# Loading the first two sequences in rows, loading layer weights behind the first projections, and a new order of units

## The chip, the core and the metric

The kernel runs on one core of a Trainium2 chip. A core has TensorE (PE, matmuls; PEld is its weight load), VectorE (DVE), ScalarE (ACT), GpSimd (POOL) and SyncE (SP), which run side by side and wait for one another through semaphores. Here SP and ACT issue all DMAs, each in its own program order. The metric is the device time of one execution in microseconds; the kernel before took 3423.85 us (median of 3 runs, 3422.1 to 3424.76).

## The reference

The inputs are 32 sequences `x` and 32 side sequences `fside`, each 256 tokens by 256 features, and a length per sequence. All is float32.

```
# conditioning: cross attention, 16 heads of 16
q = (fside + b_self) @ Wq + bq
k = concat(x + b_prev, fside + b_self) @ Wk + bk
v = concat(x, fside) @ Wv + bv
score of q against x's keys, masked by the length; one more score: q with its own key
y = (softmax(scores / 4) over both @ v) @ Wo + bo
# two layers, 8 heads of 64, local windows of 128
h = shift(y); q, k, v = split(h @ wqkv)
q, k = l2norm(q) * q_scale, l2norm(k) * k_scale, turned by rotary tables
y = y + local_attention(q, k, v) @ wo
h = layernorm(shift(y)) * lg + lb;  a, g = split(h @ w1 + b1)
y = y + (a * gelu(g)) @ w2 + b2
out = x + y
```

`shift` takes the second half of the features from the token before.

## The kernel before, in words

**Tiling.** Two sequences make a group (`G` = 2), so there are 16 groups. Activations lie with features on the 128 partitions and tokens along the row. `stream` (two buffers, L766) holds the running `y` of a group with a column of zeros in front, so that the shift is an offset.

**Stages of a group.** The loop at the end of `tile_kernel` makes, for each group and each of its sequences: `load_sequence` (L697) with `blocks` (L691), which loads `fside` and `x` with four DMAs each in blocks of 32 by 32, whose runs are 128 bytes; `prepared` (L874), which turns the two tiles on VectorE (stream transposes, 32 by 32), projects q, k, the own score and the values (`cq`, `ck`, `cs`, `vals`, `self`), and spreads q and k over the partitions into `qh` and `kh` by eight DMAs each (`spread`, L889), with four small DMAs for the mask (`behind`); `conditioned` (L945): scores `S`, their maxima `mx` on VectorE (16 reductions a sequence), the maxima turned (`nmT`) and written into `qh` as rows, transposed scores `ST`, exponentials `eT` on ACT, the weighted values `AV`, then `ohT`, `at` on POOL, `turn` and `co`. Then twice `attention` (L1042; `q`, `k`, `v`, `qkT`, `sc`, `ex`, `exT`, `av`, `wout`) and `feedforward` (L1226; `mean`, `var`, `rs`, `w`), and `finished` (L1334), which adds `x` and stores. `S`, `ST`, `sc` and others use PE in tiles of 32 or 64 rows; `AV`, `av` and some others in tiles of 32 or 64 columns; some matmuls are cut into halves or quarters of their columns (`parted`, L543) so that PE need not change its tile size.

**Weights.** Before the loop all weights are loaded on ACT's queue: the conditioning's (`wq`, `wk`, `wv`, biases, the table `misc` with the identity `ident`, L704 to L723), then sequence 1 (L769), then `wo` and both layers (L773 to L844). The layers' part also multiplies the rotary table `rope0` with the scales into `rope1`, `rope2` (VectorE), copies the ends of `w1` into `w1t` (POOL), and adds `lb @ w1` to `b1` by matmuls with one column (`b` on PE, tile `pb`, 44 rows of the trace a layer).

**What sets the order.** The code does not issue instructions as it runs. Each engine call is recorded as a node (`Plan.record`, L233), matmuls in units (`unit`, L194) with their tiles of five pools (SBUF `t2`, `t4`, `e6`, `sm`, and the eight PSUM banks) . `Plan.run` (L294) then simulates the engines with written costs and picks, whenever PE is free, the ready unit with the lowest score (`policy`, L1399). The score contains the unit's `stand`: its group times 215, its place, and a shift from the tables `SHIFT`, `FIRST` (group 0) and `FINAL` (the last two groups), which were found by search. The other engines take the ready node by `rank` (L538), that is by the time it became ready. `issue` (L552) writes the instructions in that order; they all carry line 567. So a new table or a new cost moves instructions throughout the program. A DMA's cost in the plan is its issue, its bytes on a shared wire and a landing of 2.2 us.

Of the kernel before, what the change touches and what calls it, by code (L numbers as in the profile page):

```python
# [19 lines left out]
P = 128  # L20
S = 256
D = 256
G = 2
# [3 lines left out]
FH, FD = 8, 64  # L27
# [130 lines left out]
class Plan:  # L158
# [15 lines left out]
    def __init__(self, tc, engines, pools, make):  # L174
        self.tc, self.engines, self.pools, self.make = tc, engines, pools, make
        self.nodes, self.units, self.unit_, self.group, self.place = [], [], None, 0, 0.0
        self.stage, self.stages, self.done = 0, {}, set()


    def tile(self, pool, name, shape):  # L180
# [113 lines left out]
    def run(self, policy):  # L294
# [13 lines left out]
        for u in self.units:  # L308
            for tiles in u.takes.values():
                for t in tiles:  # L310
                    t.lead = u.cost if t.lead is None else t.lead
                tiles.sort(key=lambda t: t.lead)
        self.idle = self.switches = self.cold = self.wire = 0.0

        def put(n):
            if n.engine == "PE":
# [40 lines left out]
        while todo:  # L357
# [12 lines left out]
            if e != "PE":  # L370
                ready = [n for n in waiting[e] if n.ready <= t]
                n = min(ready, key=lambda n: self.rank(n, e))
                waiting[e].remove(n)
                cost = n.cost
                if e == "S" and n.table not in ("any", None, self.table):
                    self.table, cost = n.table, cost + 1.3
                now[e] = t + cost
                if not n.load:
                    self.backlog[e] -= n.cost
                order.append(n)  # L380
                todo -= 1
                end = t + cost
                if n.load:
                    self.wire = max(self.wire, end) + n.load
                    end = self.wire + self.LANDING
                ended(n, end)
                continue
            fit = {u: fits(u) for u in units if u.ready <= t}
# [148 lines left out]

    def rank(self, n, e):  # L538
        other = e == "S" and n.table not in ("any", None, self.table)
        return n.ready + 2.0 * other, n.number  # L540


    def parted(self, u):  # L543
# [29 lines left out]
class Engine:  # L573
# [12 lines left out]


SHIFT = [
    156, 528, 54, -76, 49, 292, -28, 245, 120, -102, -425, 52, -30, 35, 68, 22, 33, 22, -208,
    -4, 119, -41, 61, 69, 90, 152, 19, 32, -62, -238, 52, -2, 49, -168, 13, -85, -54, -65, 36,  # L590
    64, 112, -439, -349, -167, 223, -408, -5, 62, -46, -234, 56, -27, 119, -7, -45, 96, -17,
    -38, 61, -374, -335, -58, 1, -150, -372, -152, -51, -265, -409, 8, 67, -53, 114, -41, -17,
    -83, 34, 68, 48, 60, -261, -99, -7, -76, -335, -100, -105, -191, -306, -58, 15, -102, 32,
    -23, -66, 39, -309, -188, 106, -258, 33, -30, -139, 22, -141, 82, -290, -255, 32, 19, -99,
    134, 126, 14, -15, -222, -574, -156, 97, 93, -32, -241, 50, 152, -118, -41, -45, 21, -102,
    20, 47, 3, 15, 55, 169, -56, -24, 43, 199, -247, 143, -97, -15, -223, -41, -95, -88, -212,
    -127, -29, -32, -285, -545, -142, -265, -8, -118, -6, 152, 84, -122, 25, 14, 4, 18, 141, 60,
    166, -454, -139, 25, -127, -186, -20,
]
FIRST = [  # L600
    0, 0, 0, 0, 0, 0, 0, 0, 10, 35, -9, 213, 102, 95, 210, -345, -65, -122, -290, 49, -201, 6,
    -193, -61, -7, 106, 99, -6, -100, -16, 106, 13, 65, -266, -137, 7, -58, 247, 58, 69, 48, 1,
    -114, -155, -32, -173, -34, 65, 135, 130, -117, 69, 71, 117, 272, 156, 73, -3, -1, -31, -33,
    -133, 51, 151, 175, 239, 445, 215, 231, 120, 135, 97, -3, -90, -188, -357, -32, -64, -276,
    -297, -374, -330, -535, -346, -72, -135, -217, 156, 27, 182, 40, -174, -48, 77, -252, -118,
    -307, -246, 33, -96, -400, -238, -150, -69, -239, 6, 79, 152, 26, -38, -60, -358, -15, -155,
    89, -99, -69, -60, 87, -3, -114, -222, -118, 60, -143, -246, -29, -171, -319, -115, -49,
    -17, -96, -75, -88, 113, 144, -56, -6, 35, -9, -141, -41, -74, -183, -115, -131, -49, -79,
    109, -65, -145, 55, -88, -244, -157, -153, -264, -181, -118, -121, -82, -23, -37, -86, -83,
    -110, -213, -219, -209, -160, -63, 0, 0,  # L610
]
FINAL = [
    0, 0, 0, 0, 0, 0, 0, 0, 56, -34, 24, 16, 12, 140, -55, -63, -14, 1, -33, -84, -66, -53, -46,
    -145, -40, -121, 67, -19, -32, -29, 98, 97, 8, 45, -119, -130, -61, -106, 67, 94, -33, 8,
    54, 33, 8, -94, -222, -47, -210, -95, -90, -11, -121, 156, 49, 10, 43, 87, 7, 64, -144, -81,
    35, -80, 47, -31, -76, -182, 53, 86, 32, 67, 229, 49, 115, 31, 6, -10, -135, 40, 27, -79,
    -83, -8, 108, -110, 63, -40, -249, -98, -95, -18, -170, -139, -28, -12, -41, 76, 83, 116,
    59, -9, 65, -157, -74, -50, -119, -145, -16, -25, 13, 6, 73, -2, -181, -184, -151, -49, -97,
    116, -8, 56, 187, 15, 69, -31, -42, -59, 109, 161, 193, 112, 209, 211, 117, 80, 41, 59, 77,
    -84, 136, 47, 92, -54, 145, 66, 93, 1, -60, 152, -30, 108, 108, -119, 50, -9, -29, -39, 44,  # L620
    -113, -118, -128, -103, 66, 10, -89, -27, -49, -2, -10, 53, 34, -67, -8,
]


# [1 line left out]
def tile_kernel(ctx: ExitStack, tc: tile.TileContext, a: dict, out: bass.AP):  # L626
# [64 lines left out]
    def blocks(name, src):  # L691
        t = sb2(name, P, 2, S // 32, 32)
        for i in range(4):
            ld(t[32 * i : 32 * i + 32], blocked(src)[i])
        return t

    def load_sequence(n, after=()):  # L697
        plan.unit(after=after)
        loaded[n] = [blocks(name, src[n]) for name, src in (("ft", f), ("xt", x))]

    load_sequence(0)
    plan.unit()

    def weight(name, src, cols):  # L704
        t = kept(name, (P, 2, cols))
        ld(t, src.rearrange("(c p) e -> p c e", p=P), act)
        return t

    wq, wk, wv = (weight(f"w{n}", a[f"L0_cond_W{n}"], D) for n in "qkv")

    def column(src, name, cols):

        t = kept(name, (P, cols))
        ld(t, src.rearrange("(c p) -> p c", p=P), act)
        return t
# [2 lines left out]
    b_self = column(a["L0_cond_b_self"].rearrange("a b d -> (a b d)"), "b_self", 2)  # L718
    bq = column(a["L0_cond_bq"], "bq", 2)
    bk = column(a["L0_cond_bk"], "bk", 2)  # L720
    bv = kept("bv", (P, D))
    ld(bv, a["L0_cond_bv"].partition_broadcast(P), act)
    ld(misc, a["c_misc"][:, 0:C_IOTA], act)  # L723

    lens_i = kept("lens_i", (B, 1), I32)
    ld(lens_i, a["itok_B_18_1004"].rearrange("(b c) -> b c", c=1))
# [39 lines left out]
    stream = [kept(f"stream{i}", (P, 2, G, S + 1)) for i in range(2)]  # L766
    for t in stream:
        vec.memset(t[:, :, :, 0:1], 0.0)
    load_sequence(1)  # L769

    plan.unit()  # L773
    wo = weight("wo", a["L0_cond_Wo"], D)
    bo = column(a["L0_cond_bo"], "bo", 2)
    rope0 = sb2("rope0", P, 2, 4, FD)
    ld(rope0, a["c_rope"].rearrange("(t p) j d -> p t j d", p=P), act)
    wqkv, wout, w1, w1t, w2, rope, lg, lb, b1, b2 = ([] for _ in range(10))
    full = HID // P
    last = HID - full * P  # L780
    for l in range(DEPTH):
        wqkv.append(weight(f"wqkv{l}", a["L0_ffn_wqkv"][l], 3 * INNER))
        r = kept(f"rope{l + 1}", (P, 2, 4, FD))
        h = FD // 2
# [57 lines left out]
        for i in range(2):  # L842
            part = b1[l][:, i, 0 : NJ - i]
            vec.tensor_tensor(part, part, pb[:, i, 0 : NJ - i], ALU.add)  # L844

    def projected(name, w, j, src):
        plan.unit()
        pm = bank(name, P, S)
        for c in range(2):
            pe.matmul(  # L850
                pm,
                lhsT=w[:, c, j * P : (j + 1) * P],
                rhs=src[:, c, :],
                start=(c == 0),
                stop=(c == 1),
            )
        return pm
# [16 lines left out]
    def prepared(n, b):  # L874

        ft, xt = loaded.pop(n)
        plan.unit()
        fT, xT = sb2("fT", P, 2, S), sb2("xT", P, 2, S)
        for dst, src in ((fT, ft), (xT, xt)):
            vec.transpose(dst.rearrange("p c t -> p (c t)"), flat(src))  # L880
        for i in range(4):
            r = 32 * i + CD
            ld(
# [464 lines left out]
    for p in range(NG):  # L1348
        plan.group, plan.place = p, 0.0
        res = stream[p % 2]  # L1350
        heads, done = [], []
        for b in range(G):
            plan.stage = (p, 1 + b)
            n = G * p + b
            if n > 1:
                load_sequence(n, gates[p - 1][b : b + 1])
            heads.append(prepared(n, b))
        for b in range(G):
            plan.stage = (p, 3 + b)
            done.append(conditioned(b, *heads[b], res))  # L1360
        gates.append(done)
        for b in range(G):
            plan.stage = (p, 5, b)
            attention(0, b, res)
        plan.stage = (p, 6)
        feedforward(0, res)
        for b in range(G):
            plan.stage = (p, 7, b)
            attention(1, b, res)
        plan.stage = (p, 8)  # L1370
        late = feedforward(1, res)
        for b in range(G):
            plan.stage = (p, 9 + b)
            finished(G * p + b, b, res, (late,))
# [77 lines left out]
```

## Time and profile before

| | us |
|---|---|
| median of the runs | 3423.85 |
| the profiled execution | 3422.27 |
| its span, first to last instruction | 3420.5 |
| PE busy, of the span | 3348.6 |
| PE busy in the first 100 us | 73.30 |
| PE busy from 430 to 3000 us | 2550.82 of 2570 |
| PE busy from 3400 us to the end | 9.04 of 20.5 |
| mean granted PE clock, all; first 100 us | 0.990; 0.76 |
| DVE, ACT, POOL busy | 2161.9, 1780.5, 1163.4 |

The page gives the busy time of each engine, and the span in 40 equal slices with the busy share in tenths, the clock that PE was granted in tenths of full speed, and the DMA engines' share. A view of the waits names the waiting instruction, who released it, the total, the number of times and the longest. A view by windows gives busy time and number of instructions of PE, PEld, DVE, ACT and POOL in a stretch, then the clock, the DMA share and GB/s. A view in order of time gives start, duration, engine, operation, output and inputs, and how often in a row; queue names such as ACTq and SPq stand for the issue of a DMA. A float32 matmul has two rows in the trace, a transpose one; their ends are modelled, so what a row costs is read from the start of one to the start of the next.

### The profile page before, as it was taken

How to read it: one execution, taken by the hardware profiler on the slowest of the kernel's cores; microseconds unless marked ns; L12 is line 12 of the kernel's file. 1: busy time of each engine (PE TensorE's matmuls, PEld its weight loads, DVE VectorE, ACT ScalarE, POOL GpSimd, SP SyncE). 2: the span in 40 equal slices, each digit the busy share in tenths (PEclk: the TensorE clock that was granted, in tenths of full speed). 3: DMA queues.
4: the chain of work that ended last, by engine and by line, in shares of the span. 5: the costliest groups of instructions: out<-in, count | busy, mean ns of one | idle time of the engine just before them, and what ended most of it. 6: DMA issues, size and time to landing. Idle time of an engine off the chain costs nothing.

```text
span 3420.5 us, 69279 instructions
## 1 busy us (share of the span) xinstructions
PE 3348.6 (98%) x25984; PEld 1908.7 (56%) x25984; DVE 2161.9 (63%) x6673; ACT 1780.5 (52%) x4537; POOL 1163.4 (34%) x1195
## 2 busy tenths in 40 slices
PE   6999999999999999999999999999999999999998
PEld 5665556465564655656455564655646556465554
DVE  3558567485675747657485674847657486574763
ACT  0556456473554726456373563735547364554653
POOL 0325052250613407043160522507134070432541
PEclk7999999999999999999999999999999999999999
DMA  5100010010101001010010100101010010100001
GB/s 147 20 15 11 12 27 9 16 26 9 26 15 21 17 13 20 16 20 17 13 21 14 27 13 15 24 7 26 16 20 17 13 20 15 27 15 12 4 2 27
DMA packets 310926, 69.00 MB, mean 20 GB/s; under 512 B 286776, under 2 KB 308096, under 8 KB 310592
## 3 DMA queue, kind: packets, MB, share of 16 engines
q1 hardware_dynamic: 298848, 54.24, 9.3%
q10 hardware_dynamic: 11744, 10.34, 1.1%
q8 instruction: 207, 3.39, 0.4%
q14 instruction: 127, 1.04, 0.1%
HBM read 35.53 MB, written 8.39 MB: 13 GB/s over the span
## 4 chain that ended last, share of the span: by engine, by line
PE 77%; DVE 12%; POOL 3%; ACT 1%; issue 1%; POOLq 0%; SPq 0%; DMA 0%; DVEq 0%; ACTq 0%
PE w L567 27%; DVE ex L567 6%; PE wout L567 6%; PE q L567 5%; PE av L567 4%; PE k L567 4%; PE sc L567 4%; PE S L567 4%; PE v L567 3%; PE ST L567 3%; PE vals L567 3%; PE AV L567 3%; PE exT L567 2%; PE qkT L567 2%; DVE rot L567 2%; PE cs L567 2%
## 5 line engine op out<-in xcount | busy, mean ns | idle before, releaser
L567 ACT ACTIVATE ex<-ex,nm,rq 128x128 f32<-128x128 f32 (+1 forms) x1024 | 546.2, 537 | 107.3 <-DVE nm L567 106.1
L567 PE MATMUL w<-cen,w 128*128 128x512 f32 (+2 forms) x1480 | 589.2, 598 | 0.8 <-DVE cen L567 0.3
L567 POOL TENSOR_TENSOR raw<-raw,rot 128x512 f32<-128x512 f32 x256 | 327.6, 1281 | 749.2 <-DVE rot L567 660.3
L567 PEld LDWEIGHTS w<-cen,w 128*128 128x128 f32 (+2 forms) x1480 | 224.9, 175 | 270.7 <-issue 231.4
L567 DVE TENSOR_SCALAR ex<-ex,den 128x128 f32<-128x128 f32 (+1 forms) x1024 | 351.4, 457 | 5.2
L567 DVE TENSOR_REDUCE mx<-S 128x2 f32<-128x512 f32 x512 | 314.3, 686 | 49.4 <-PE S L567 49.3
L567 PE MATMUL w<-act,w 128*128 128x512 f32 (+3 forms) x880 | 324.6, 602 | 2.9 <-DVE act L567 2.8
L567 ACT ACTIVATE eT<-ST 128x512 f32<-128x512 f32 x512 | 263.8, 605 | 115.0 <-PE ST L567 109.8
L567 DVE CUSTOM_DVE_ANT_0 ex<-sc,misc 128x128 f32<-128x128 f32 (+1 forms) x1024 | 299.2, 353 | 31.3 <-PE sc L567 30.8
L567 DVE SCALAR_TENSOR_TENSOR act<-w,b,act 128x512 f32<-128x512 f32 (+1 forms) x192 | 143.4, 748 | 262.0 <-PE w L567 195.5
L567 ACT ACTIVATE act<-w,b 128x512 f32<-128x512 f32 (+1 forms) x192 | 128.9, 686 | 280.1 <-PE w L567 276.8
L567 POOL TENSOR_TENSOR xs<-stream 128x512 f32<-128x512 f32 x32 | 35.0, 1094 | 641.5 <-PE cs L567 318.1
L567 PE MATMUL wout<-qT,wout 128*64 128x256 f32 (+2 forms) x1728 | 242.8, 381 | 0.5 <-DVE nm L567 0.3
L567 PE MATMUL v<-wqkv,stream 128*128 128x512 f32 (+1 forms) x608 | 242.5, 599 | 0.0
L567 PE MATMUL k<-wqkv,stream 128*32 128x512 f32 (+2 forms) x1104 | 239.9, 593 | 0.0
L567 PE MATMUL q<-wqkv,stream 128*32 128x512 f32 (+2 forms) x960 | 237.7, 594 | 0.2 <-ACT stream L567 0.2
L567 ACT COPY exT<-exT 128x384 f32<-128x384 f32 x512 | 207.3, 498 | 54.5 <-PE exT L567 53.8
L567 PEld LDWEIGHTS w<-act,w 128*128 128x128 f32 (+3 forms) x880 | 124.8, 176 | 167.1 <-issue 151.5
L567 POOL TENSOR_TENSOR rq<-ss,minus_half 128x8 f32<-128x8 f32 x128 | 215.1, 1684 | 4.9
L567 POOL TENSOR_TENSOR ss<-ss,minus_half 128x8 f32<-128x8 f32 x128 | 213.3, 1666 | 5.7
L567 PE MATMUL sc<-kT,qT 64*128 64x128 f32 (+1 forms) x2048 | 205.7, 337 | 0.4
L567 PEld LDWEIGHTS wout<-qT,wout 128*64 128x64 f32 (+2 forms) x1728 | 161.6, 147 | 73.0 <-issue 17.6
(127 smaller groups left out, 5520.2 us busy)
## 6 DMA issues: line engine op xcount, KB each, us to landing
ft<-in_fside_BxSxS_dram SPq DMA_DIRECT2D x128, 64.0 KB
xt<-in_x_dram SPq DMA_DIRECT2D x128, 64.0 KB
qh<-qc SPq DMA_DIRECT2D x256, 32.0 KB
kh<-kc SPq DMA_DIRECT2D x256, 32.0 KB
ot<-in_x_dram SPq DMA_DIRECT2D x128, 64.0 KB
out_dram<-ot SPq DMA_DIRECT2D x128, 64.0 KB
wqkv<-in_L_ffn_wqkv_dram ACTq DMA_DIRECT2D x2, 1536.0 KB
w<-in_L_ffn_w_dram ACTq DMA_DIRECT2D x2, 1364.0 KB
```

Source lines behind the costliest of these rows:

```text
L567: ins = getattr(self.engines[n.engine], name)(*[real(v) for v in args], **{k: real(v) for k, v in kw.items()})
```

## The change

Sequences 0 and 1 (`n < G`) are loaded by one DMA for each tensor, in rows of 1 KB, and turned by PE (`turned_tiles`, four 128 by 128 transposes and a copy) instead of VectorE. The identity is loaded by a DMA of its own ahead of the other weights; `wv`, `bv` and the rest of `misc` come behind the small biases; sequence 1 is requested before the mask's inputs. Each layer's weights are recorded by a new function `load_layer(l, after)`, called for layer 0 behind the recording of sequence 0's projections and for layer 1 behind those of sequence 1, and with an edge that lets the plan start them only after these; `rope0` is loaded once for each layer. `wo` and `bo` are recorded behind this. In the plan a DMA now also waits for the landing of the one eight loads before it (`landed`), and `rank` has a term with the factor `hurry`, which the kernel sets to `HURRY` = 0.0 as before. The three tables of shifts are replaced; the number of units in group 0 has grown.

```diff
@@ Plan.run
+        self.landed = [0.0] * 8
...
                 if n.load:
-                    self.wire = max(self.wire, end) + n.load
+                    at = max(t, self.landed[-8]) + cost
+                    now[e] = at
+                    self.wire = max(self.wire, at) + n.load
                     end = self.wire + self.LANDING
+                    self.landed.append(end)
@@ Plan.rank
-        return n.ready + 2.0 * other, n.number
+        return n.ready + 2.0 * other + self.hurry * n.unit.stand, n.number
@@ SHIFT, FIRST, FINAL: other numbers throughout
@@ tile_kernel
+    def rows(name, src):
+        t = sb2(name, P, 2, D)
+        ld(t, src.rearrange("(t p) d -> p t d", p=P))
+        return t
     def load_sequence(n, after=()):
         plan.unit(after=after)
-        loaded[n] = [blocks(name, src[n]) for name, src in (("ft", f), ("xt", x))]
+        shape = rows if n < G else blocks
+        loaded[n] = [shape(name, src[n]) for name, src in (("ft", f), ("xt", x))]
     load_sequence(0)
     plan.unit()
+    ld(ident, a["c_misc"][:, C_ID : C_ID + P], act)
...
-    wq, wk, wv = (weight(f"w{n}", a[f"L0_cond_W{n}"], D) for n in "qkv")
+    wq, wk = (weight(f"w{n}", a[f"L0_cond_W{n}"], D) for n in "qk")
...
     bk = column(a["L0_cond_bk"], "bk", 2)
+    wv = weight("wv", a["L0_cond_Wv"], D)
     bv = kept("bv", (P, D))
     ld(bv, a["L0_cond_bv"].partition_broadcast(P), act)
-    ld(misc, a["c_misc"][:, 0:C_IOTA], act)
+    ld(misc[:, P:C_IOTA], a["c_misc"][:, P:C_IOTA], act)
+    load_sequence(1)
+    plan.unit()
...
-    load_sequence(1)
-    plan.unit()
-    wo = weight("wo", a["L0_cond_Wo"], D)
-    bo = column(a["L0_cond_bo"], "bo", 2)
-    rope0 = sb2("rope0", P, 2, 4, FD)
-    ld(rope0, a["c_rope"].rearrange("(t p) j d -> p t j d", p=P), act)
...
-    for l in range(DEPTH):
+    def load_layer(l, after):
+        plan.unit(after=after)
+        rope0 = sb2("rope0", P, 2, 4, FD)
+        ld(rope0, a["c_rope"].rearrange("(t p) j d -> p t j d", p=P), act)
         wqkv.append(weight(f"wqkv{l}", a["L0_ffn_wqkv"][l], 3 * INNER))
...
+    plan.unit()
+    wo = weight("wo", a["L0_cond_Wo"], D)
+    bo = column(a["L0_cond_bo"], "bo", 2)
@@ prepared
         ft, xt = loaded.pop(n)
-        plan.unit()
-        fT, xT = sb2("fT", P, 2, S), sb2("xT", P, 2, S)
-        for dst, src in ((fT, ft), (xT, xt)):
-            vec.transpose(dst.rearrange("p c t -> p (c t)"), flat(src))
+        if n < G:
+            fT, xT = turned_tiles("fT", ft), turned_tiles("xT", xt)
+            plan.unit()
+        else:
+            plan.unit()
+            fT, xT = sb2("fT", P, 2, S), sb2("xT", P, 2, S)
+            for dst, src in ((fT, ft), (xT, xt)):
+                vec.transpose(dst.rearrange("p c t -> p (c t)"), flat(src))
@@ the loop over groups
             heads.append(prepared(n, b))
+            if p == 0:
+                plan.stage = (-1, 1 + b)
+                load_layer(b, (plan.unit_,))
```

`turned_tiles` is in the kernel before (L859), where `conditioned` uses it for `at`.

## The prediction

> **What bounds the kernel now.** I read the page first, then what the engines waited for in the first 100 us, then the start in stretches of 2 us, then the start in order of time.
>
> ```profile
> span 3420.5 us, 69279 instructions
> ...
> PE 3348.6 (98%) x25984; PEld 1908.7 (56%) x25984; DVE 2161.9 (63%) x6673; ACT 1780.5 (52%) x4537; POOL 1163.4 (34%) x1195
> ...
> PE   6999999999999999999999999999999999999998
> ...
> PEclk7999999999999999999999999999999999999999
> DMA  5100010010101001010010100101010010100001
> ```
>
> TensorE (PE) is the bound, and only the first and the last slice leave it idle. Idle is 3420.5 - 3348.6 = 71.9 us: the stretches 0 to 100 and 430 to 3000 us show 73.30 and 2550.82 us busy, so 26.7 us of it fall in the first 100 us, 19.2 us in the 2570 us of the middle, and 11.5 us in the last 20.5 us. Nearly all that an edit of the start can win is in the first 100 us, whose waits are these:
>
> ```profile
> PE cq L567 <- DVE fT L567: 9.1, 1, 9.1
> PE bias L567 <- DMA bq<-in_L_cond_bq_dram: 7.8, 1, 7.8
> PE S L567 <- DMA w<-in_L_ffn_w_dram: 4.5, 1, 4.5
> PE S L567 <- DMA kh<-kc: 2.9, 1, 2.9
> PE self L567 <- DVE prod L567: 2.4, 2, 1.7
> ```
>
> Each line: who waited for what, total us, times, longest. The 9.1 us is for sequence 0 turned on VectorE, and the 7.4 us of "S" is for `qh` and `kh`, which SyncE spreads by 16 DMAs. The second loss there is the clock:
>
> ```profile
> 44.00:46.00 2.00, 2.00 (x10) 1.97 (x10) 0.00 (x0) 0.00 (x0) 0.00 (x0) 0.50 0.83 264
> 46.00:48.00 2.00, 0.06 (x1) 0.00 (x0) 0.27 (x2) 0.00 (x0) 0.00 (x0) 0.50 0.99 346
> 86.00:88.00 2.00, 2.00 (x20) 1.71 (x24) 0.74 (x2) 0.00 (x0) 0.00 (x0) 0.50 0.00 0
> ...
> 108.00:110.00 2.00, 2.00 (x12) 1.17 (x11) 0.00 (x0) 1.94 (x5) 0.00 (x0) 0.54 0.44 70
> ```
>
> The third number from the end is the granted clock: one half at 44 us although PE is busy throughout (matmuls with one column, for the b1 bias), and again at 86 us.
>
> **The front, part by part.** These rows of the start in order of time (start, us, engine, what, how many) give the prices:
>
> ```profile
> 22.09 3.78 PE L567 MATMUL cq<-fT,wq 128*128 128x256 f32 x8 [9.05 <-DVE fT L567]
> 25.67 1.32 PE L567 MATMUL vals<-wv,xT 128*128 128x256 f32 x4
> ...
> 33.71 0.39 ACTq L567 DMA_DIRECT2D wqkv<-in_L_ffn_wqkv_dram  x1
> ...
> 36.53 8.67 PE L567 MATMUL b<-lb,w 128*128 128x1 f32 x40
> ...
> 43.83 10.41 SPq L567 DMA_DIRECT2D kh<-kc  x8
> ...
> 70.22 5.03 SPq L567 DMA_DIRECT2D qh<-qc  x8
> ```
>
> *Loads in rows.* Removed: 16 DMAs of 32x16x32 (runs of 128 B) and four stream transposes of 0.66 to 0.71 us. Added: 4 DMAs of the shape of `wq`, which was issued at 0.72 and had released the next user of its semaphore at 3.98. The changed order puts them first on SP, so sequence 0 is there at about 4 us instead of 20. PE gets 16 transposes; 128 such rows in 22.4 us (turn) is 0.175 each: +2.8 us with their tails, 1.75 at the 109 ns from one to the next. VectorE gets four copies of 0.69 (aT<-turn), where it is idle. Both hide in the 7.8 us before "bias", which waits for `b_self`; that load is now issued at about 3.6 (behind the small `ident` load) and took 4.7 us before, so bias starts at 8.5, not 7.8, and takes the 5.3 us it took: 14 us. Then `cq` follows at once, not at 22.09: **8 us won here**.
>
> *Both sequences projected together.* 40 matmuls of 128x256 are 80 rows; four matmuls took 3.78 us at the slow start, others 0.216 us a row: 3.8 + 72 x 0.216 = 19.4, and two `self` units 1.8. PE has no more of this at 35 us. The first `spread` is of sequence 1: `qc` is complete at 21.3, then 8 + 4 + 8 DMAs at 0.63 (5.03 for 8, unloaded). But the 18th of them waits for a semaphore that the `rope` load took before it, and ACT issues that only behind its eighth projection copy, at 33.4; with the 3 us of a `wq` this gives 36.5, and with two more DMAs and 3.8 us of landing (the last `kh` issue ended at 54.24, S went on at 58.06), S starts at **41 us** (before: 50.60). PE idles 6 us for it.
>
> *The layers' weights later.* From the issue of `wqkv` to `w1` landed took 33.71 to 50.77 = 17.1 us for layer 1, and `w2` another 5.2. In the new order `wqkv` of layer 0 goes at 34.4, so `w1` lands at 51.5 and `w2` at 57. In the changed order a DMA of either queue waits for the one eight places before it, so the spreads of sequence 0 stand among these loads: its fifth `kh` waits for `w2`'s first part, two `qh` for b1 parts, one for the second `rope`. So SP goes on at 57, needs 10 more DMAs and a landing: S of sequence 0 at 67 us. Layer 1 follows: `w1` at 59.4 + 17.1 = 76.5, ACT free at 78.
>
> *What stands until ST.* S of sequence 1: 16 reductions `mx` at 0.62 from one to the next, from 43.2: 53, then 12 small rope products (1.5 us, which now stand before `nm`) and `nmT` at 55. The b1 bias of layer 0, 44 rows at one half: 8.67 + 0.99, so 9.5: 64.7. S of sequence 0 from 67: 2.2 + 9.8 + 1.5, `nmT` at 80.5. The bias of layer 1, 9.5 more, since PE stood nearly idle before: **ST starts at 90 us**. The kernel before starts ST at 85.88 with one S unit (1.15) and one `vals` unit (1.9 at full clock) still to do: 88.9. So the 8 us won at 14 us are spent by 90: VectorE paces both S blocks, and nothing but the bias lies beside them. **Front +1 us.** Ends: -9 if both bias units ran as at 69.24 (4.52 + 0.62) and S came sooner; +10 if the spreads land as late as under load (10.41 for 8).
>
> The Trainium skill, "TensorE: Matmul & The Clock Gate", Part 1 (The HAM clock gate), says that some 3.4 us of sustained matmuls bring the full clock. By it the bias units would be at full clock after that time, and ST would start some 5 us sooner. The row at 44 us differs: 8.7 us of one-column matmuls stayed at 0.50 to their end, so the sum goes by the row.
>
> *ST and AV of both sequences in one block.* Before, 86 to 118 us lost 1.9 us idle and 7.7 by the clock (4 in 86 to 94, 0.3, then 0.9 + 2 + 0.5 in 108 to 116). Now 8 ST and 8 AV units alternate in pairs: 128 rows each at 152.5/2048 and 143.6/2048 = 18.5 us of PE beside 32 exponentials at 263.8/512 = 16.5 us of ACT. I take half of the ST units at half clock (+4) and 2 us of waits: **-4 us** (-9 to +4: all at half clock).
>
> **The order anew, middle.** Counting the changed order of instructions: 63 of 1064 changes of tile size go (a 128x512 matmul is followed after 522 ns, not 429, by another tile size: 63 x 0.093 = -5.9). But `self` and `var` are cut less often into halves: 8 to 19 and 6 to 18 whole units, each about 0.5 us dearer (self: 9.0/8 against 13.8/23): +11. The 512 exT units stand 0.3 us further behind their scores than before, where 11 waits of 0.5 us stood: -4; `wout`, `vals`, `k` in larger tiles -3. **-2 us**, ends -8 and +13 (below).
>
> **The end.** Between 3000 and 3400 us PE waited 6.7 us, 2.8 of it for `act`, 1.6 at the last norm, where only two matmuls covered POOL's 1.02 us. The new order has three there, and no `w2` unit nearer than 1.7 us behind its `act` (before 0.8). After the last matmul the same 11.4 us follow: two VectorE adds, four transposes, POOL, eight output DMAs. **-2 us** (-5 to +3).
>
> Sum: +1 - 4 - 2 - 2 = -7. The profiled execution took 3422.27 us (span 3420.5 and 1.8 around it): 3415. Its runs have a median of 3423.85, 1.6 above: **3417 us**.
>
> **Rivals.** *Slower: the wait at `turn`.* PE now reaches `turn` 3.3 us of PE work behind `ohT` in 11 groups, before 4.4, and there `turn <- POOL at` waited 11 times 0.25 us (2.8 of the middle's waits). If POOL is as late as before, each costs 1.1 more: +12, and with the front at +5: 3433. It decides when `at` ends over 3.3 us after `ohT`. For it: the wait of each group is in the trace. Against: POOL was busy with other work until that `at`, and its order is new. *Slower: the load chain is late.* If each of the three waits of SP on `w2`, b1 and `rope` takes 5 us more, S of sequence 0 comes at 82 and ST at 105: +15, 3432; it decides from S after 75 us. For it: `kh<-kc` took 10.41 us beside weights and 5.77 us at 64.35, alone. Against: in the layer-1 stretch the weights took what I already count. *Given back:* the front stays +1, the ST block runs at half clock throughout, the middle is even: 3423. *Clock full in S and bias:* -9 in the front: 3407; for it the bias at 69.24, which ran behind 8 us of dense matmuls, against it the row at 44 us. That the rows do not hasten the first projection can hardly be: 4 DMAs stand where 16 stood.
>
> **How the numbers follow.** Forecast (3411 to 3421) 0.46; clock full 0.18; given back 0.13; `turn` 0.12; late chain 0.11. A measurement of this kernel can tell about 0.2% from no change, 6.8 us: faster is below 3417.0, slower above 3430.7. Of the forecast 0.28 lies below and 0.18 above; so faster 0.28 + 0.18 = 0.46, same 0.18 + 0.13 = 0.31, slower 0.23. The range, 3402 to 3433, leaves out the lower ends of front and middle together and the two slow rivals together.
>
> **What would show it.** `cq` at 14 us, S at 41, second S at 67, ST at 90; the clock one half in both bias units; the waits of the first 100 us on `fT` gone and new ones on `kh` and `mx`; `turn <- POOL at` below 0.5 us a group. Wrong if ST starts before 80 or after 100 us, or if the middle's idle time leaves 12 to 27 us.

## The result, and the profile after

The changed kernel takes 3458.18 us (median of 4 runs, 3456.87 to 3459.23), the kernel before beside it 3423.47. The ratio is 1.0101, 95% interval 1.0084 to 1.0119: slower by 35 us, where 3417 was forecast. The profiled execution took 3457.14 us. From the page of the changed kernel (its helper's line is 572 now):

```profile
span 3455.3 us, 68870 instructions
...
PE 3367.3 (97%) x25834; PEld 1935.2 (56%) x25834; DVE 2187.3 (63%) x6690; ACT 1774.0 (51%) x4516; POOL 1166.8 (34%) x1195
...
PEclk7999999999999999999999999999999999999999
```

In slices of 86 us nothing is to be seen; the loss is spread thin. The front first: the waits of PE in the first 100 us, then the front in order of time.

```profile
PE nmT L572 <- DVE nm L572: 8.1, 2, 4.3
PE S L572 <- DMA kh<-behind: 6.6, 2, 5.7
```

```profile
14.20 2.05 PE L572 MATMUL cq<-fT,wq 128*128 128x256 f32 x4
...
59.89 8.53 PE L572 MATMUL b<-lb,w 128*128 128x1 f32 x40
...
92.39 3.79 PE L572 MATMUL ST<-qh,kh 18*128 18x256 f32 x32
```

The front runs as it was worked out: `cq` at 14, the second S (of sequence 0) at 69, ST at 92, and PE idles 22.1 us in the first 100 where it idled 26.7. The waits from 430 to 3000 us are another matter:

```profile
PE wout L572 <- DVE qT L572: 29.0, 11, 2.7
PE turn L572 <- POOL at L572: 8.9, 11, 0.8
```

The first did not exist before; the second was 2.8 us:

```profile
PE turn L567 <- POOL at L567: 2.8, 11, 0.3
```

One of the eleven waits of `wout`, in stretches of 2 us (PE busy first, third number from the end the clock):

```profile
1152.00:1154.00 2.00, 0.34 (x4) 0.27 (x6) 2.00 (x5) 0.32 (x1) 0.65 (x1) 1.00 0.00 0
1154.00:1156.00 2.00, 2.00 (x12) 0.96 (x10) 2.00 (x5) 0.00 (x0) 0.99 (x1) 0.55 0.00 0
1156.00:1158.00 2.00, 2.00 (x6) 0.26 (x4) 2.00 (x6) 0.00 (x0) 1.92 (x3) 0.59 0.03 8
```

PE stands idle for 2.6 us (from 1151.0), and then, from 1154.2, works 3.4 us at half clock, which costs 1.7 us more. That happened behind five of the eleven waits. From the first ST of one group to that of the next it is 209.0 or 210.4 us, where the kernel before had 207.2.

**Where the 34.8 us of span are** (idle time by the windows; lost to the clock is PE's busy time times what is missing from the full clock, over stretches of 2 us):

| us | idle before | after | lost to the clock before | after |
|---|---|---|---|---|
| 0 to 430 | 33.9 | 27.2 | 25.1 | 27.1 |
| 430 to 3000 | 19.2 | 43.1 | 0.0 | 8.5 |
| 3000 to the end | 18.8 | 17.7 | 1.6 | 4.9 |
| sum | 71.9 | 88.0 | 26.7 | 40.5 |

Idle is +16.1, the clock +13.8, and some 5 us are left as work. The middle alone accounts for 32.4.

**What makes the wait.** The changed kernel around it in order of time (start, us, engine):

```profile
1142.44 1.53 PE L572 MATMUL sc<-kT,qT 64*128 64x128 f32 x16
...
1145.20 1.27 POOL L572 TENSOR_TENSOR raw<-raw,rot 128x512 f32<-128x512 f32 x1
1145.23 1.25 DVE L572 SCALAR_TENSOR_TENSOR nm<-nm,rq 128x4 f32<-128x4 f32 x1
...
1146.52 0.49 ACT L572 ACTIVATE ex<-ex,nm,rq 128x128 f32<-128x128 f32 x1 [2.60 <-DVE nm L572]
...
1146.86 0.16 DVE L572 SCALAR_TENSOR_TENSOR nm<-nm,rq 128x4 f32<-128x4 f32 x1
...
1148.27 1.64 POOL L572 TENSOR_TENSOR ss<-ss,minus_half 128x8 f32<-128x8 f32 x1
...
1150.12 2.98 DVE L572 TENSOR_SCALAR ex<-ex,den 128x128 f32<-128x128 f32 x4
1150.28 1.27 POOL L572 TENSOR_TENSOR raw<-raw,rot 128x512 f32<-128x512 f32 x1 [0.38 <-DVE rot L572]
1151.51 1.14 POOL L572 TENSOR_TENSOR raw<-raw,ss 128x512 f32<-128x512 f32 x1
1152.94 0.67 DVE L572 COPY qT<-av 128x512 f32<-128x512 f32 x1
...
1153.66 1.48 PE L572 MATMUL wout<-qT,wout 128*64 128x256 f32 x8 [2.64 <-DVE qT L572]
```

Read it upwards. `wout` waits for the copy of `av` into `qT`. The copy stands in VectorE's queue behind four scalings of the other sequence's `ex`. These take 2.98 us; rows of their two kinds (128 and 256 columns) take 0.33 and 0.47 at the median, but the second here took 1.52 and the third 1.13, and they end 0.3 and 0.1 us behind the two POOL instructions. The small product `nm` by `rq`, earlier, took 1.25 us beside a POOL sum; the next one, beside POOL's power (the 1.67 us of `rq`, which raises 8 columns to the power -1/2), took 0.16. So VectorE is held by some of what POOL does, and what stands behind it is late.

The Trainium skill, "SBUF — State Buffer", section "Who interferes with whom", has this as a rule: a VectorE instruction in a mode that uses two ports, which `tensor_scalar` can enter, wants the port pair that GpSimd uses, and so does one with two inputs in SBUF against a GpSimd instruction that reads SBUF; the one that comes second waits for the whole of the other. The product that starts 0.03 us behind the sum and ends 0.01 us behind it (1146.48 and 1146.47) agrees.

The middle as a whole shows it too. From 430 to 3000 us, 81 scalings and `nm` products began with more than 0.6 us left of a POOL instruction of 512 columns, and all 81 took over 30% and 0.1 us more than their median; 60 began so beside one of 4 or 8 columns, nearly all powers, and none of them did.

### The profile page after: what moved, and what is told of

The parts are those of the page before. It is cut to its first block, busy times and chain, and to the rows that moved or that the text cites. A ratio compares the mean times of both kernels' runs of the same rounds, so it can differ in the third digit from the quotient of the medians.

```text
span 3455.3 us, 68870 instructions
## 1 busy us (share of the span) xinstructions
PE 3367.3 (97%) x25834; PEld 1935.2 (56%) x25834; DVE 2187.3 (63%) x6690; ACT 1774.0 (51%) x4516; POOL 1166.8 (34%) x1195
## 4 chain that ended last, share of the span: by engine, by line
PE 83%; DVE 11%; POOL 2%; ACT 2%; DMA 1%; SPq 1%; issue 1%; POOLq 0%; DVEq 0%; ACTq 0%
PE w L572 27%; PE wout L572 6%; PE q L572 6%; PE v L572 5%; DVE ex L572 5%; PE ST L572 4%; PE av L572 4%; PE S L572 4%; PE sc L572 4%; PE k L572 4%; PE AV L572 4%; PE vals L572 3%; PE exT L572 3%; PE qkT L572 2%; PE cs L572 2%; PE ck L572 1%
## 5 line engine op out<-in xcount | busy, mean ns | idle before, releaser
L572 DVE TENSOR_SCALAR ex<-ex,den 128x128 f32<-128x128 f32 (+1 forms) x1024 | 361.9, 466 | 5.7
L572 PE MATMUL wout<-qT,wout 128*64 128x256 f32 (+1 forms) x1520 | 242.4, 383 | 29.8 <-DVE qT L572 29.0
L572 PE MATMUL k<-wqkv,stream 128*32 128x512 f32 (+2 forms) x968 | 248.7, 609 | 1.9 <-DVE rot L572 1.7
L572 PE MATMUL v<-wqkv,stream 128*32 128x512 f32 (+2 forms) x932 | 243.1, 596 | 0.3 <-DVE nm L572 0.3
L572 PEld LDWEIGHTS wout<-qT,wout 128*64 128x64 f32 (+1 forms) x1520 | 168.5, 156 | 106.9 <-DVE qT L572 34.3
```

The source lines that it names most:

```text
L572: ins = getattr(self.engines[n.engine], name)(*[real(v) for v in args], **{k: real(v) for k, v in kw.items()})
```

## The experiments

Theory at the start: the eleven waits and the clock behind them are the loss, made by VectorE's order and its collisions with POOL. Rivals: VectorE is simply full there, so that the wait moves; or the front costs it. "Period" is the time from one group's first ST to the next one's.

**1. The copy of qT first.** In the order that the plan hands to `issue`:

```diff
     order = plan.run(policy)
+    for copy in [VectorE's copies qT <- av]:
+        first = the first of the scalings ex <- ex, den that stand directly ahead of it
+        order.remove(copy); order.insert(order.index(first), copy)
```

> Only VectorE's order is edited: in the 11 groups where the copy of av into qT, on which wout waits, stands behind the four scalings of the other sequence's weights (ex by den), it is put ahead of them. Theory: these 11 waits are what the changed kernel lost in the middle: 29.0 us of idle time and 8.6 us of clock behind every second one. The copy then ends at about 1150.8 us of the span where wout wants it at 1151.0, so the wait goes: 3458 - 29 - 8.6 = 3420 us, granted clock 1.00 from 430 to 3000 us, `turn` waits unchanged at 8.9. Rival 1, VectorE is the bound there and the wait only moves on to exT or qkT: 3450 to 3458. Rival 2, the loss sits in the front (weights loaded late): at least 3445.

Measured: 3454.2 us, ratio to before 1.0089 (1.0070 to 1.0108). The waits from 430 to 3000 us:

```profile
PE exT L572 <- DVE ex L572: 21.7, 11, 2.0
```

The wait of `wout` is gone, and a new one stands at `exT`, 1.97 us long and again with half the clock behind five of eleven. Rival 1 was right about this edit: the copy was late because VectorE was late, not because of its place.

**2. Two POOL instructions less.**

```diff
+    for copy in [the same 11 copies]:
+        drop POOL's raw <- raw, rot and raw <- raw, ss that stand beside the scalings
```

> Leaves out, in the same 11 groups, the two GpSimd instructions that stand beside the scalings: the sum of raw and rot, and the product of raw with ss, of one half of k (22 instructions; those k go unturned and unscaled into the scores). VectorE's order is that of the changed kernel. Theory: two of the four scalings take 1.5 and 1.1 us in place of 0.45 and 0.33 because they wait for GpSimd's instruction to end; without it the four take 1.15 in place of 2.98, the copy of qT comes 1.8 us earlier and the wait of wout falls from 2.64 to about 0.8 us, too short to cost the clock: 3458 - 11 x 1.8 - 8.6 = 3429.5 us. Rival, the scalings are long for another reason, or the order in VectorE's queue alone makes the wait: 2.64 us stays, 3455 to 3459.

Measured: 3436.5 us, ratio 1.0041 (1.0029 to 1.0054).

```profile
1146.25 1.13 DVE L572 TENSOR_SCALAR ex<-ex,den 128x128 f32<-128x128 f32 x4
...
1147.94 1.08 PE L572 MATMUL wout<-qT,wout 128*64 128x256 f32 x8 [0.77 <-DVE qT L572]
```

The four scalings take 1.13 us, the wait falls to 0.77, no clock is lost from 430 to 3000 us, and the period is 207.8. So POOL holds VectorE, and 21.7 us of the loss hang on these two instructions a group (28.5 were expected; where the other 7 stay is open).

**3. Both late places on VectorE.** The wait of `turn` has the same form. In the changed kernel:

```profile
1122.29 0.74 DVE L572 COPY kT<-qkT 128x256 f32<-128x256 f32 x2
...
1122.95 0.41 DVE L572 TENSOR_TENSOR tv<-tv,ohT 128x256 f32<-128x256 f32 x1
...
1123.44 0.62 POOL L572 TENSOR_TENSOR at<-tv,den 128x256 f32<-128x256 f32 x1 [1.13 <-DVE den L572]
...
1124.12 0.55 PE L572 MATMUL turn<-misc,at 128*128 128x128 f32 x3 [0.81 <-POOL at L572]
```

```diff
+    the edit of 1, and
+    for tv in [VectorE's sums tv <- tv, ohT]:
+        put it ahead of the copies qT, kT <- qkT that stand directly ahead of it
```

> The edit of the copy of qT, and a second one of the same kind: on VectorE the sum tv + ohT is put ahead of the four copies out of qkT that it stands behind in 11 groups; `at` on GpSimd and `turn` on TensorE wait for it. Theory: the 0.8 us waits of turn go too, 6 us more than the first edit alone: 3414 us, idle time of TensorE from 430 to 3000 below that of the kernel before (19.2 us), clock 1.00. Rival, each wait that is taken away is replaced by another on the same VectorE: 3420 or more. Against the kernel before (3423.5) the theory gives 0.3% less.

Measured: 3423.4 us, ratio 0.9998 (0.9987 to 1.0008): 31 us less than with the copy alone, for a wait of 8.8. That did not fit independent waits. `exT` now waited 0.7 us, so by number and by place the rival held (3420 or more, another wait); the period was 206.4.

**4. The sum tv + ohT alone.** Only the second half of that edit.

> The changed kernel with the move of tv + ohT alone; wout's copy stays behind the scalings. If the two waits are independent: 6 to 8 us less than the changed kernel, 3450 us, wout's wait 2.6 us. If the collisions with GpSimd depend on how VectorE and GpSimd stand to each other, and this move changes that (with both moves the product nm by rq took 0.34 us, with the copy's move alone 1.22): VectorE comes some 0.9 us earlier to the copy, wout waits 1.7 to 1.9 us, and with the clock partly kept the time is 3434 to 3442 us.

Measured: **3416.3 us**, ratio 0.9975 (0.9965 to 0.9985). Not one wait of `wout` is left, although its copy still stands behind the scalings, and the period is 206.0. Here is the same place:

```profile
1135.05 1.53 PE L572 MATMUL sc<-kT,qT 64*128 64x128 f32 x16
...
1137.84 0.33 DVE L572 SCALAR_TENSOR_TENSOR nm<-nm,rq 128x4 f32<-128x4 f32 x1
1138.32 1.29 POOL L572 TENSOR_TENSOR raw<-raw,rot 128x512 f32<-128x512 f32 x1
...
1138.55 1.07 DVE L572 SCALAR_TENSOR_TENSOR nm<-nm,rq 128x4 f32<-128x4 f32 x1
...
1141.39 1.65 POOL L572 TENSOR_TENSOR ss<-ss,minus_half 128x8 f32<-128x8 f32 x1
1141.81 1.16 DVE L572 TENSOR_SCALAR ex<-ex,den 128x128 f32<-128x128 f32 x4
...
1142.99 1.29 POOL L572 TENSOR_TENSOR raw<-raw,rot 128x512 f32<-128x512 f32 x1
```

Count both from the start of the scores `sc` (1142.44 in the changed kernel, 1135.05 here). The product `nm` comes at +2.79 in both. POOL's sum comes at +2.76 there and holds it; here at +3.27, behind it. The sum has not become harmless: here it holds the next product, 1.07 us in place of 0.16. But ACT can already begin with what the first product gave. So the exponentials follow at +4.08 there and +3.16 here, the scalings at +7.68 and +6.76. Here they are done (+7.92) when POOL's next sum begins (+7.94); there they meet it. Both sides of my expectation were too small: it is one chain, and half a microsecond decides it.

**5. One collision less, everything else as in the changed kernel.**

```diff
+    for n in [POOL's raw <- raw, rot beside VectorE's nm <- nm, rq, 11 times]:
+        n.ops = [("tensor_tensor", (spare, mean_w[:, 0:6], minus_half[:, 0:6], ALU.pow), {})]
```

> The changed kernel with its order, but in the 11 groups the GpSimd sum of raw and rot that runs beside VectorE's product nm by rq (1.25 us there in place of 0.16) is left out, and a power of 6 columns stands in its place, which takes GpSimd about as long and has the same neighbours (one half of k's raw keeps its unturned part). Theory, that one collision sets off the rest: without it the exponentials and the scalings come 0.9 us earlier and run beside GpSimd's power of 1.65 us instead of beside its sum, take 1.15 in place of 2.98 us, and wout's wait of 2.64 goes whole: 3458 - 29 - 8.6 = 3420 us, turn's waits unchanged at 8.9. Rival 1, a power holds VectorE as the sum does, or the scalings still meet the sum: wout waits 1.7 us or more, 3436 us or more. Rival 2, it was turn's wait itself that held wout, not the collision: 3455 or more.

Measured: 3425.3 us, ratio 1.0003 (0.9994 to 1.0013).

```profile
1140.61 1.37 POOL L572 TENSOR_TENSOR spare<-mean_w,minus_half 128x6 f32<-128x6 f32 x1
1140.65 0.19 DVE L572 SCALAR_TENSOR_TENSOR nm<-nm,rq 128x4 f32<-128x4 f32 x1
...
1144.47 1.16 DVE L572 TENSOR_SCALAR ex<-ex,den 128x128 f32<-128x128 f32 x4
```

The scalings are as short as in 4. The waits of `turn` are all there (9.5 us), those of `wout` all gone, the clock full from 430 to 3000 us, the period 206.7. So the collision of the first `nm` with the sum is the link between the two waits; with 4, where the sum came half a microsecond later against `sc` once `turn` no longer waited, it says that `turn`'s 0.8 us does its harm by shifting PE and VectorE against POOL. All ten runs (3421.96 to 3426.58) lie above the 3420 expected: the period fell by 3.0 us, where the wait and its clock make 3.4, and I can't account for the rest.

**6. The clock alone.**

```diff
+    for n in [wout's first unit behind the same 11 copies]:
+        n.ops = [first matmul of n, complete in itself] * 5 + n.ops
```

> The changed kernel with its waits of wout left in place, but filled: wout's first product is made five times more (11 x 5 matmuls into its own bank, overwritten by the real sum), some 2.2 us of TensorE work where it idles for 2.64. If the clock's 8.6 us follow from TensorE being idle for 2.6 us, the clock stays at 1.00 behind every wait and the time falls by them although not one wait has been taken away: 3449.5 us. If the low clock behind every second wait has another cause (what runs after the wait), it stays: 3458 us, or up to 3463 if the filler itself comes late.

Measured: 3448.4 us, ratio 1.0071 (1.0051 to 1.0091). The time fell by 10 us by giving PE more to do: no clock was lost from 430 to 3000 us, every period was 209.1.

**7. Front or order?** First the new front with the old tables (each unit with the shift that it had), then the old front with the new tables.

> The new front (rows, TensorE turns, late layer weights, the planner's model of a full DMA queue) with the tables of the kernel before, each unit with the shift that it had there. Theory, the new order is what lost the time and the front is about even: the middle comes back to the period of the kernel before, 207.2 us in place of 209.75, no wait of wout for qT, and the whole is between 3415 and 3435, according to how badly tables found for another front fit the first groups. Rival, the front costs what was lost: 3450 or more.

> The kernel before (old front, old model of the loads) with the new tables, each unit with the shift that it has in the changed kernel. Theory, the waits of wout belong to the tables, not to the front: the middle has the changed kernel's period, 209 to 210 us with a wait of 2.6 us for qT in every group (the first groups can be worse, since these tables were found for the other front; the whole 3450 to 3500 us). Rival, the waits come from the new front's later start or its model of the loads: a period of 207 to 208 us, no waits of wout.

Measured: 3474.8 us (ratio 1.0151, 1.0129 to 1.0173) and 3556.7 (1.0385, 1.0371 to 1.0399). With the old tables the middle was indeed back at 207.2 to 208.0 without waits of `wout`, but the first groups had lost 44 us by the second layer of group 2. With the new tables on the old front neither side came true: no waits of `wout`, and periods of 212.8 to 218.3 us in the later groups, after longer ones (one of 222.9, one of 259.5). So in both runs the tables did worse away from the front and the cost model for which they were found, and which of the three put the sum behind the copies stays open.

**8. A third move, and the front.** Three moves on VectorE (the next scalings ahead of raw, rot and ss of k); then these with a changed front:

> Both moves of the last kernel, and a third on VectorE in the same 11 groups: the next four scalings of ex stand ahead of raw, rot, rot and ss of k, for which exT waited 0.7 us. If the rest of the loss is again only this place in VectorE's queue: 7.7 us less than with two moves, 3416 us, a period of 205.7 us, and 0.2% below the kernel before. Rival, the collision with GpSimd's product of raw and ss holds the scalings wherever they stand (they begin 1.8 us earlier but the first waits for GpSimd until 1150.1): the wait stays near 0.5 us and the time near 3421.

> As the last one, but the loads of the second layer and `rows` stay where they were: only the bias matmuls are moved. If the bias alone held S and ST, the same 3407 us. If loads and `rows` on ACT's queue hold them anyway (the spread of q issued until 66 us, `rows` at 79 us), ST starts near 84 us and the bias work at full clock eats what that gives: 3414 to 3418 us.

> The three moves in the middle, and the front: the 13 large loads of the second layer's weights are issued after the first scores instead of ahead of them on ACT's queue, `rows` of the first sequence stands ahead of them (before, it waited on ACT until 79 us behind those loads), and the column matmuls of both layers' b1 bias (8.5 + 1.0 us each at half clock, between S and ST) are cut into pieces of 4 and put between full matmuls later on. Theory, S and ST of the front are held by work and loads put ahead of them, which nothing needs yet: ST starts near 75 us in place of 92, the bias comes back as 2 x 4.7 us at full clock, so 8 to 9 us less than with the three moves alone: 3407 us. Rival, the weights of the second layer are then late, or S waits for its own spread of q and k through the same DMA queues: no gain, 3416 or more.

Measured: 3426.7, 3427.2 and 3422.1 us (ratios 1.0005, 1.0009, 0.9997, each within 0.001). The third move gained nothing: the waits went on to `sc` (11.6 us in three kinds), period 206.9. In the front ST started at 92.5, 83.3 and 76.6 us. Of the 16 us that the last one won, `var` of the first layer saw 6 and that of the second 1.4: the bias came back at full clock with some 5 us a layer, and the rest I can't account for. With the two moves of 3 instead of three:

> The front of e7 (second layer's loads, `rows` and bias moved) with the two moves of e3 in the middle and without the third, which made the period 206.9 us in place of 206.4. Expected from the sum of the two: 3423.4 - 4.6 = 3419 us, 0.2% below the kernel before, period 206.4 us. Rival: the front's gain of e7 over e5 is chance of the clock's windows, and the time is that of e3, 3423 us.

Measured: 3416.3 us, ratio 0.9975 (0.9966 to 0.9984).

**9. Keeping the clock in the front.**

```diff
+    def warm(n, out, times):
+        n.ops = [("matmul", (out,), {"lhsT": mean_w, "rhs": wq[:, 0, :], ...})] * times + n.ops
+    warm(each of the first two nmT units, its own bank, 5); warm(first ST unit, its own bank, 5)
```

> As e9, with 15 matmuls of 128 rows by 256 columns into banks that are overwritten, five ahead of each of the first two nmT and five ahead of the first ST, where TensorE idles for 4.3, 3.8 and 2.3 us. Theory: S and ST of 17 and 18 rows cannot raise the clock by themselves but keep it once raised, so S of the second sequence takes 5 us in place of 9.7 and ST and AV after it start at full clock: 6 to 16 us less than e9. Rival: S lets the clock fall again whatever came before it, or the filler's own half-clock time (0.86 us each) fills the waits and no more: as e9, up to 3 us more.

Measured: 3413.4 us, ratio 0.9967 (0.9954 to 0.9979).

```profile
60.88 2.08 PE L572 MATMUL S<-kh,qh 17*128 17x256 f32 x22
63.13 6.52 PE L572 MATMUL S<-kh,qh 17*128 17x256 f32 x42 [0.17 <-DMA qh<-qc]
```

The filler did raise the clock, to 0.95 and more from 60 to 66 us where it had been 0.50. But S goes at 95 ns a row for 22 rows only, and then at 155, about as at half clock (152 in the changed kernel): VectorE's 16 reductions, 0.62 us from one to the next, pace it, and from 67 us on the clock is 0.50 again. My 5 us for S forgot VectorE, which the prediction had named as what paces S. 3 us were won rather than 6 to 16.

**10. Everything that helped.** The front of 9 with the one move of 4.

> The front of e12 (second layer's loads, `rows` and bias moved, 15 matmuls that keep the clock) with the one move of e11 in the middle (tv + ohT first) and no other. Sum of the two: 3413.4 - 11 x 0.4 = 3409 us, period 206.0 us, 0.45% below the kernel before. Rival: the phase that e11 found is lost again when the front ends earlier, a wait comes back in each group: 3420 us or more.

Measured: **3407.9 us** (median of 5, 3406.35 to 3412.86), ratio 0.9955 (0.9942 to 0.9967), as expected (3409): below both kernels.

## Why the prediction was wrong

*The front* (+1, and -4 for the block of ST and AV): right, with ST 2 us late. `cq` at 14 was 14.20, S at 41 was 40.99, S of sequence 0 at 67 was 69.20, ST at 90 was 92.39; both bias units ran at half clock, 8.53 + 0.99 us, as the row said and against the rule that was weighed. From ST's start to 118 us PE lost 0.4 us idle and 3.6 by the clock, where 6 were forecast and 9.7 were lost before. Idle time to 430 us fell by 6.7 us, the clock took 2.0.

*The middle* (-2): this is the step that failed. It counted changes of tile size and distances between a matmul and its inputs' producers in PE's order. It had no term for the producers' own time, as if a scaling took its 0.33 or 0.47 us and a product its 0.16 in any order, and it put no price on what stands ahead of a producer in VectorE's queue, nor on which POOL instruction runs beside it. The middle measured +32.4 instead: 11 waits of `wout` of 2.64 us (29.0), 6.1 more at `turn`, 8.5 of clock, less what other waits gave back. The waits of `wout` came from the four scalings that POOL stretched from 1.16 to 2.98 us, behind a product stretched from 0.16 to 1.25. Without the chain (experiment 4) the new order is better than I said: period 206.0 against 207.2 us, some 13 us over eleven groups.

*The rival at `turn`* had the right place and the wrong size. It priced 1.1 us a group; 0.81 less 0.25 was lost there. It stopped at the wait itself. Experiments 4 and 5 show what the price should have been: 0.8 us, plus what a shift of half a microsecond between VectorE and POOL sets off 20 us later, 2.64 us, plus the clock.

*The end* (-2): idle -1.1, clock +3.3, so +2.2; the sum had no term for the clock there.

*The test that I set* ("wrong if the middle's idle time leaves 12 to 27 us") gave the answer at once: 43.1. The trace of before held the warning. In its middle, scalings and `nm` products already stood 51 us above their own medians (rows more than 30% and 0.1 us above it), mostly beside POOL's sums of `raw` and `rot`, but no wait of PE there was put down to a scaling, and those put down to `nm` came to 3.4 us; after the change it is 81.

## What to carry to other kernels

A new order that no cost model has seen collide must be read for pairs: for two engines that hold each other up, as VectorE and GpSimd do here, lay the rows of both beside each other where a third one waits. A periodic wait cost here its length times the periods, and more where TensorE's clock fell behind it, and the wait to take away first was here the earliest small one of the period, not the longest. These tables belonged to the model and the front for which they were found; carried over, they lost 51 and 131 us.

## What the runs showed of the hardware

- GpSimd holds VectorE by what it does, not by how long: beside the sum of 128x512 (1.27 us) a product of four columns took 1.25 us; beside a power of 6 columns (1.37 us) it took 0.19, and beside one of 8 (1.65 us) four scalings took 1.16, where they took 1.13 without POOL's pair (experiment 2). In the middle of the changed kernel it was 81 of 81 beside 512 columns and 0 of 60 beside 4 or 8. No run tells the kind of instruction from its few columns. The Trainium skill, "SBUF — State Buffer", section "Who interferes with whom", says that the pair is held for the whole instruction and makes no exception for these; here the measurement decides.
- A gap of 1.97 or 2.64 us in TensorE's work cost the clock behind five of eleven, 3.4 us of half clock each time; gaps of 0.8 us in the same stretch (`turn`, and `wout` in experiment 2) never did, nor did the long gap once it was filled (experiment 6). The Trainium skill, "TensorE: Matmul & The Clock Gate", section "Why this matters for your kernels", asks for no gaps above some 3 us; these runs put the danger lower.
- Matmuls with 17 of 128 rows, at VectorE's pace of some 155 ns a row, did not raise the clock: S of sequence 0 was busy for 9.7 us at 0.50. Raised by full matmuls before, the clock stayed up for some 6 us of S and then fell (experiment 9). Whether the few rows or the pace keep it low, no run tells.
